# Attention with the output projection folded into the value weights on the chip

## The chip, the cores and the metric

The kernel runs on one core of one Trainium2 chip. The metric is the device time of one execution in microseconds; the median of three runs is given. Profiles come from one further execution, recorded by the hardware profiler. TensorE is written PE (its weight loads PEld), VectorE DVE, ScalarE ACT, GpSimd POOL and SyncE SP, as the profile has them. A matmul of 32-bit numbers leaves two records in the trace.

## The reference

The program is four layers on an image x of 48 channels and 128 x 128 points; each layer normalises x in groups of three channels, computes something and adds it to x. Only the first layer is touched:

```python
def _L0_conv_ref(x, qkv_w, dw_w, proj_w, temperature):
    qkv = jnp.einsum('bchw,oc->bohw', x, qkv_w)
    qkv = jax.lax.conv_general_dilated(qkv, dw_w, window_strides=(1, 1), padding='SAME', feature_group_count=3 * c, ...)
    q, k, v = jnp.split(qkv, 3, axis=1)
    q, k, v = (tok(q), tok(k), tok(v))          # 16384 tokens of 48 channels
    q = _l2norm(q)
    k = _l2norm(k)
    attn = jnp.einsum('bnc,bmc->bnm', q, k) * temperature
    attn = jax.nn.softmax(attn, axis=-1)
    out = jnp.einsum('bnm,bmc->bnc', attn, v)
    out = out.transpose(0, 2, 1).reshape(b, c, h, w)
    return jnp.einsum('bchw,oc->bohw', out, proj_w)
```

x becomes x plus this, of the normalised x. The other layers are recurrent sweeps over the image, a layer with Fourier transforms of 8 x 8 patches, and a state-space scan over tokens. The projection is linear in v, and v is linear in the value weights; the division by the softmax's sum is one number for each query.

## The kernel before

Everything is 32-bit. The layers run one after the other (`tile_kernel`). The image stays in SBUF in two large tiles, xa and xb; in attention xa holds the image and then the queries, and xb holds the keys k and the values v.

**Setup and convolution** (`attention`). The channels are laid out with a gap: 48 channels lie in rows 0 to 31 and 33 to 48 of 64 (GAP is 49), so that row or column 32 can hold ones. Line 129 builds proj, 128 x 112, from two DMAs (lines 131 to 133): in each half of 64 rows the projection stands in columns 0 to 47, and row 32, which carries the sum of the softmax, has ones in columns 64 to 111. `packed_weights` (line 106) multiplies 1x1 weights and 3x3 weights into one tile wt, 128 partitions, four groups, 192 columns: 64 each for q, k, v. Then VectorE takes the statistics of x (line 155). The convolution runs in eight bands of 16 rows, each in two steps of eight rows: `band` normalises on VectorE and places shifted copies by DMAs on SP, `conv` multiplies on TensorE, and `take` divides q and k by their norms and turns v by transposes through PSUM tile pt. Line 269 copies v out on VectorE; GpSimd writes ones into row 32 of k (line 272) and column 32 of v (line 273).

**Attention** (`attend`, chosen at run time for a small temperature; `attend_shifted` is the other branch and isn't run with these inputs). Queries go in 32 chunks of 512 (variable c), keys in 64 steps of two tiles of 128 (variable j). `scores` issues four matmuls, each in a quarter of the array, into one of three PSUM buffers s, and ScalarE takes the exponential into e. `sums` multiplies e with v, again four quarters of 64 columns, into acc, which has one buffer. Sums stand two steps behind their scores (BEHIND). The operations of TensorE and ScalarE are kept in the order of the program by the wrapper `InOrder`, which is why all of them carry line 48 in the profile; VectorE, GpSimd and SP are ordered by the scheduler of the kernel language.

**A chunk end** (class `Finish`) has two parts. When the last sums of a chunk are issued, `__init__` loads the residual xres by SP (line 357), copies acc to o on ScalarE, and adds the two halves of its free dimension on VectorE into osum (line 361). The two halves of partitions are still separate. In the next chunk, after the step j = 6, `result` multiplies proj with osum: that one product adds the halves of partitions, projects, and spreads the softmax's sum over 48 rows. Its output takes a turn of the buffers s. ScalarE copies it to y, and VectorE takes the reciprocal (line 369), multiplies (370), adds the residual (371) and takes the statistics for the next layer (372); SP stores x1 (373). After the last chunk `result` follows `__init__` at once, and the next layer, `sweeps`, begins with the statistics.

Of the kernel before, what the change touches and what calls it, by code (L numbers as in the profile page):

```python
# [19 lines left out]
F32 = mybir.dt.float32  # L20
# [6 lines left out]
C = 48  # L27
H = W = 128
N = H * W
CH = 512  # L30
GAP = 49
# [68 lines left out]
def packed_weights(nc, pool, name, w, dw, cols):  # L100

    w1 = pool.tile([128, 4, cols], F32, name="w1")
    nc.scalar.dma_start(w1.rearrange("c t o -> c (t o)"), w)
    wt = pool.tile([128, 4, cols], F32, name=name)
    nc.scalar.dma_start(wt.rearrange("c t o -> c (t o)"), dw)
    nc.vector.tensor_mul(wt, wt, w1)
    return wt
# [6 lines left out]
def attention(ctx, tc, xq, other, x1, const, ins):  # L114


    nc = tc.nc
    ident, blk, st = const["ident"], const["blk"], const["st"]
# [3 lines left out]
    kv = ctx.enter_context(tc.tile_pool(name="l0_kv", bufs=1))  # L122

    k = other[:, 0:HALF]

    v = other[:, HALF:N].rearrange("p (t c) -> p t c", c=64)


    proj = kv.tile([128, 64 + C], F32, name="proj")
    nc.vector.memset(proj, 0.0)  # L130
    for b in (0, 64):
        nc.sync.dma_start(proj[b : b + GAP, 0:C], ins["l0_proj"])
        nc.vector.memset(proj[b + 32 : b + 33, 64:], 1.0)
    temp = kv.tile([128, 1], F32, name="temp")
    nc.sync.dma_start(temp, ins["l0_temp"].to_broadcast([128, 1]))

# [3 lines left out]
    absT = kv.tile([128, 1], F32, name="absT")  # L140
    nc.vector.tensor_mul(absT, temp, sgn)

    with ExitStack() as a:
# [6 lines left out]


        wt = packed_weights(nc, wp, "wt", ins["l0_w"], ins["l0_dw"], 192)

        for i in range(NQ):
            nc.vector.bn_stats(st[:, i, :], xq[0:C, i * CH : (i + 1) * CH])
# [79 lines left out]
        def take(t0, p, pv):  # L235

            sqs, psss, nrms = [], [], []
            for n in range(2):
                sqs.append(sp.tile([128, CH], F32, name="sq"))
                act.activation(sqs[n], p[n], AF.Square)  # L240
            vt = sp.tile([128, CH], F32, name="vt")
            act.copy(vt, pv)

            for n in range(2):
                psss.append(ps2.tile([128, CH], F32, name="pss"))
                pe.matmul(psss[n], lhsT=blk, rhs=sqs[n], start=True, stop=True)
                nrms.append(sp.tile([128, CH], F32, name="nrm"))
                act.activation(nrms[n], psss[n], AF.Sqrt)
            pt = ps1.tile([128, 4, 2, 64], F32, name="pt")
            for i in range(4):  # L250
                pe.transpose(
                    pt[:, i].rearrange("t n c -> t (n c)"), vt[:, i * 128 : (i + 1) * 128], ident
                )
            kb = 64 * (t0 // HALF)
            tk = t0 % HALF
            left = []
            for n in range(2):
                nc.vector.tensor_scalar_max(nrms[n], nrms[n], 1e-12)
                rn = sp.tile([128, CH], F32, name="rn")
                nc.vector.reciprocal(rn, nrms[n])  # L260
                q = slice(t0 + n * CH, t0 + (n + 1) * CH)
                nc.vector.scalar_tensor_tensor(
                    xq[0:64, q], p[n][0:64], sgn[0:64], rn[0:64], ALU.mult, ALU.mult
                )
                left.append(q)
                nc.vector.tensor_mul(  # L266
                    k[kb : kb + 64, tk + n * CH : tk + (n + 1) * CH], p[n][64:128], rn[64:128]
                )
            nc.vector.tensor_copy(
                v[:, t0 // 128 : t0 // 128 + 8, :].rearrange("t (n i) c -> t i n c", n=2), pt  # L270
            )
            nc.gpsimd.memset(k[kb + 32 : kb + 33, tk : tk + 2 * CH], 1.0)
            nc.gpsimd.memset(v[:, t0 // 128 : t0 // 128 + 8, 32:33], 1.0)
            return left

        cur = band(0)
# [17 lines left out]
    small = nc.values_load(absT[0:1, 0:1].bitcast(mybir.dt.int32))  # L294
    bits = int(np.float32(32.0).view(np.int32))
    with tc.If(small <= bits) as near:
        attend(tc, xq, k, v, x1, proj, absT, st, ins)
    with near.Else():
        attend_shifted(tc, xq, k, v, x1, proj, absT, ident, st, ins)


@with_exitstack
def attend(ctx, tc, xq, k, v, x1, proj, absT, st, ins):

    nc = tc.nc
    act, pe = InOrder(tc, nc.scalar), InOrder(tc, nc.tensor)  # L310
    NQ = N // CH
    KT = N // 2 // 128
    BEHIND = 2

    ep = ctx.enter_context(tc.tile_pool(name="l0_e", bufs=BEHIND + 3))
    sp = ctx.enter_context(tc.tile_pool(name="l0_b", bufs=2))
    ps_s = ctx.enter_context(tc.tile_pool(name="l0_ps", bufs=3, space=PSUM))
    ps_a = ctx.enter_context(tc.tile_pool(name="l0_pa", bufs=1, space=PSUM))


    sides = [slice(0, 64), slice(64, 128)]
    quarters = [(part, half, to) for part in sides for half, to in enumerate(sides)]

    def scores(c, j):
        s = ps_s.tile([128, 2, CH], F32, name="s")
        for part, half, _ in quarters:
            b = 64 * half
            pe.matmul(
                s[part, half, :],
                lhsT=k[b : b + GAP, j * 128 + part.start : j * 128 + part.stop],  # L330
                rhs=xq[b : b + GAP, c * CH : (c + 1) * CH],
                start=True,
                stop=True,
            )
        e = ep.tile([128, 2, CH], F32, name="e")
        act.activation(e, s, AF.Exp, scale=absT)
        return e

    def sums(acc, j, e):

        for part, half, to in quarters:
            pe.matmul(
                acc[to, part.start // 64, :],
                lhsT=v[part, half * KT + j, :],
                rhs=e[part, half, :],
                start=(j == 0),
                stop=(j == KT - 1),
            )

    class Finish:  # L350


        def __init__(self, c, acc):
            self.c = c
            self.cols = slice(c * CH, (c + 1) * CH)
            self.xres = sp.tile([C, CH], F32, name="xres")
            nc.sync.dma_start(self.xres, ins["x"][:, self.cols])
            o = sp.tile([128, 2, CH], F32, name="o")
            act.copy(o, acc)
            self.o = sp.tile([128, CH], F32, name="osum")  # L360
            nc.vector.tensor_add(self.o, o[:, 0], o[:, 1])  # L361

        def result(self):
            p = ps_s.tile([128, 2, CH], F32, name="s")[0 : 64 + C, 0, :]
            pe.matmul(p, lhsT=proj, rhs=self.o, start=True, stop=True)
            y = sp.tile([64 + C, CH], F32, name="y")
            act.copy(y, p)
            rec = sp.tile([C, CH], F32, name="rec")
            nc.vector.reciprocal(rec, y[64 : 64 + C])  # L369
            nc.vector.tensor_mul(rec, y[0:C], rec)  # L370
            nc.vector.tensor_add(xq[0:C, self.cols], rec, self.xres)
            nc.vector.bn_stats(st[:, self.c, :], xq[0:C, self.cols])
            nc.sync.dma_start(x1[:, self.cols], xq[0:C, self.cols])

    waiting, finish, acc = [], None, None
    for c in range(NQ):
        for j in range(KT):
            waiting.append((c, j, scores(c, j)))

            if c and j == BEHIND:  # L380
                continue
            while len(waiting) > BEHIND:
                n, i, e = waiting.pop(0)
                if i == 0:
                    acc = ps_a.tile([128, 2, CH], F32, name="acc")
                sums(acc, i, e)
                if i == KT - 1:
                    finish = Finish(n, acc)
            if c and j == BEHIND + 4:
                finish.result()  # L390
    for n, i, e in waiting:
        sums(acc, i, e)
    Finish(NQ - 1, acc).result()


@with_exitstack
def attend_shifted(ctx, tc, xq, k, v, x1, proj, absT, ident, st, ins):

    nc = tc.nc
    NQ = N // CH  # L400
# [11 lines left out]
    k16 = k16p.tile([128, HALF], F16, name="k16")  # L412
    for i in range(0, HALF, 2048):
        nc.vector.tensor_copy(k16[:, i : i + 2048], k[:, i : i + 2048])

    class Shift:

# [45 lines left out]
    class Finish:  # L463
# [9 lines left out]

        def result(self):
            p = ps_1.tile([128, CH], F32, name="pmisc")
            nc.tensor.matmul(p[0 : 64 + C], lhsT=proj, rhs=self.o, start=True, stop=True)
            rec = sp.tile([C, CH], F32, name="rec")
            nc.vector.reciprocal(rec, p[64 : 64 + C])
            nc.vector.tensor_mul(rec, p[0:C], rec)
            nc.vector.tensor_add(xq[0:C, self.cols], rec, self.xres)  # L480
            nc.vector.bn_stats(st[:, self.c, :], xq[0:C, self.cols])
            nc.sync.dma_start(x1[:, self.cols], xq[0:C, self.cols])
# [1216 lines left out]
```

## Time and profile before

| | us |
|---|---|
| median of three runs | 7702.65 (7696.43 to 7703.76) |
| the profiled execution's own time | 7707.8 |
| its span in the trace | 7706.0 |
| setup and convolution | 0 to 257 |
| attention | 257 to 3821 |
| chunk ends in it | 32 |
| product with proj, start to start of the next | 1.04 |
| copy of acc (128 x 1024) on ScalarE | 1.00 |
| addition osum (128 x 512) on VectorE | 0.69 |
| reciprocal (48 x 512) on VectorE | 3.35 |
| exponential (128 x 1024) on ScalarE | 1.11 |

Over the whole span PE is busy for 6227.8 us (81%), DVE for 3377.0 (44%), ACT for 4455.4 (58%) and POOL for 2793.0 (36%). A line of the timeline has the start in us from the span's start, the length, the engine, the line of the code, the operation, the tiles that are written and read with the shapes, the number of instructions merged, and in brackets how long the engine was idle before and what ended that. Neighbouring instructions of a kind are merged into one line, and since matmuls overlap in the array, lines of PE overlap too; the distance of two starts is then the measure, not the length. Tile p of `result` is allocated under the name s, so that the product with proj reads `s<-osum,proj`.

### The profile page before, as it was taken

What the parts mean: (1) busy time and instruction counts of PE and PEld (TensorE: products, weight loads), DVE (VectorE), ACT (ScalarE), POOL (GpSimd) and SP (SyncE); (2) the same over time, 40 slices, a digit from 0 to 9 for tenths busy, and PEclk for the clock granted to TensorE, in tenths of its full rate; (3) what the DMA queues carried; (4) which work ended last, traced back from release to release, by engine and by line L of the source; (5) the groups of instructions that cost most, each with busy time, mean ns of one, the idle gap of its engine ahead of it and who ended that gap; (6) DMA issues with size and microseconds to landing.
All of it is one profiled execution on the core that took longest, in us unless ns stands there. A gap on an engine that the chain in (4) does not pass through costs nothing. (4 is left out here: it accounts for less than half of the span.)

```text
span 7706.0 us, 203399 instructions
## 1 busy us (share of the span) xinstructions
PE 6227.8 (81%) x93872; PEld 3159.4 (41%) x93872; DVE 3377.0 (44%) x2467; ACT 4455.4 (58%) x4928; POOL 2793.0 (36%) x573
## 2 busy tenths in 40 slices
PE   7999999999999999999888889745545554554555
PEld 2333333333333333333377755334434343434444
DVE  8300000000000000000022234489999999999998
ACT  2566666666666666666624014366666666666665
POOL 1000000000000000000000122289999999999998
PEclk9999999999999999999999999867767767676676
DMA  5000000000000000000000011166556656666775
GB/s 76 10 3 3 3 2 3 3 3 2 3 3 3 2 3 3 2 3 3 6 1 17 1 31 48 23 166 166 158 160 161 157 161 154 163 157 161 180 180 148
DMA packets 167597, 488.84 MB, mean 63 GB/s; under 512 B 33440, under 2 KB 51968, under 8 KB 163984
## 3 DMA queue, kind: packets, MB, share of 16 engines
q1 hardware_dynamic: 160704, 470.30, 24.3%
q8 instruction: 737, 12.08, 0.7%
q10 hardware_dynamic: 6032, 5.44, 0.3%
q14 instruction: 124, 1.02, 0.0%
HBM read 428.86 MB, written 22.02 MB: 59 GB/s over the span
## 5 line engine op out<-in xcount | busy, mean ns | idle before, releaser
L48 ACT ACTIVATE e<-s,absT 128x1024 f32<-128x1024 f32 x2048 | 2277.3, 1114 | 1217.9 <-PE s L48 1217.9
L1459 POOL TENSOR_TENSOR h<-du,bt 128x3072 f32<-128x3072 f32 (+1 forms) x386 | 2559.5, 6666 | 102.7 <-DMA du<-rep 70.2
L48 PE MATMUL s<-xa,xb 49*64 49x512 f32 x16384 | 2128.4, 589 | 10.6 <-DVE xb L266 10.6
L48 PE MATMUL acc<-e,xb 64*64 64x512 f32 x16384 | 2125.0, 588 | 0.0
L1466 DVE TENSOR_TENSOR_SCAN h<-dA,carry,h 128x1024 f32<-128x1024 f32 x864 | 1940.7, 2329 | 48.9 <-ACT dA L48 32.9
L48 ACT ACTIVATE dA<-dt,a 128x1024 f32<-128x1024 f32 x1152 | 1287.2, 1118 | 864.0 <-DVE h L1466 854.5
L48 PE MATMUL y<-h,cw 128*32 128x48 f32 x49152 | 899.2, 246 | 949.0 <-issue 511.9
L361 DVE TENSOR_TENSOR osum<-o 128x512 f32<-128x512 f32 x32 | 22.2, 692 | 3114.8 <-ACT o L48 3114.8
L593 POOL MEMSET xa<- 48x128 f32 x1 | 0.3, 326 | 3561.0 <-PE acc L48 3561.0
L48 PEld LDWEIGHTS y<-h,cw 128*32 128x32 f32 x49152 | 809.9, 140 | 1072.3 <-issue 661.8
L48 PEld LDWEIGHTS s<-xa,xb 49*64 49x64 f32 x16384 | 626.3, 132 | 1151.2 <-issue 615.6
L48 PEld LDWEIGHTS acc<-e,xb 64*64 64x64 f32 x16384 | 628.6, 132 | 1133.7 <-issue 1111.2
L1466 DVE TENSOR_TENSOR_SCAN h<-dA,h 128x1024 f32<-128x1024 f32 x288 | 636.1, 2272 | 44.1 <-ACT dA L48 33.6
L48 PE MATMUL yz<-ev,sel 128*8 128x48 f32 x4096 | 192.9, 260 | 277.2 <-ACT ev L48 273.3
L48 PEld LDWEIGHTS yz<-ev,sel 128*8 128x8 f32 x4096 | 162.5, 106 | 334.9 <-ACT ev L48 308.7
L657 PE MATMUL p<-xb,w 112*112 112x129 f32 x1524 | 235.7, 291 | 42.2 <-DVE xb L48 42.1
L657 PE MATMUL p<-xa,w 112*112 112x129 f32 x1524 | 233.5, 289 | 41.8 <-DVE xa L48 41.8
L678 POOL TENSOR_TENSOR xb<-xb,xa 48x2048 f32<-48x2048 f32 (+2 forms) x10 | 44.6, 4464 | 563.0 <-DVE xa L48 563.0
L657 PEld LDWEIGHTS p<-xb,w 112*112 112x112 f32 x1524 | 183.7, 178 | 93.9 <-DVE xb L48 93.9
L640 ACT COPY xa<-xb 48x128 f32<-48x128 f32 x256 | 107.4, 419 | 196.6 <-issue 138.1
L657 PEld LDWEIGHTS p<-xa,w 112*112 112x112 f32 x1524 | 181.8, 177 | 93.3 <-DVE xa L48 93.3
L369 DVE RECIPROCAL rec<-y 48x512 f32<-48x512 f32 x32 | 107.1, 3348 | 257.5 <-ACT y L48 257.5
(187 smaller groups left out, 3602.4 us busy)
## 6 DMA issues: line engine op xcount, KB each, us to landing
du<-rep SPq DMA_DIRECT2D x768, 256.0 KB
dt<-rep SPq DMA_DIRECT2D x768, 256.0 KB
rest<-xa SPq DMA_DIRECT2D x96, 77.0 KB
rest<-band SPq DMA_DIRECT2D x48, 129.9 KB
rep<-dd SPq DMA_DIRECT2D x24, 192.0 KB
yd<-ys ACTq DMA_DIRECT2D x256, 12.0 KB
band<-band SPq DMA_DIRECT2D x8, 414.4 KB
xa<-xa SPq DMA_DIRECT2D x16, 199.1 KB
```

The lines of the kernel that those rows point to most:

```text
L48: ins = method(*args, **kwargs).ins
L361: nc.vector.tensor_add(self.o, o[:, 0], o[:, 1])
L369: nc.vector.reciprocal(rec, y[64 : 64 + C])
L593: nc.gpsimd.memset(b[64:K, lines, E + W - 1 : E + W], 0.0)
L640: nc.scalar.copy(u[at : at + C, :, y], t[0:C, E + h, E : E + W])
L657: nc.tensor.matmul(p, lhsT=w[0:K, which, i, :], rhs=state[0:K, 2 * i : 2 * i + L], start=False, stop=(i == 2),)
L678: nc.gpsimd.tensor_add(xr, xr, u[0:C, x : x + xr.shape[2], E : E + H].rearrange("c w h -> c h w"),)
L1459: nc.gpsimd.tensor_mul(h[:, p, ks], du.unsqueeze(1).to_broadcast([128, ks.stop - ks.start, LC]), r["bt"][:, ks],)
L1466: nc.vector.tensor_tensor_scan(h[:, p, k, :], dA, h[:, p, k, :], carry[:, i, k : k + 1] if ci else 0.0, ALU.mult, ALU.add,)
```

## The change

The value weights are multiplied by the projection once, at the start: four transposes, a copy, four matmuls and a copy back into columns 128 to 191 of wt. Values then come out of the convolution already projected, in columns 0 to 47 without a gap, and GpSimd writes ones into columns 48 to 63. Rows 0 to 47 of acc are then the projected output and rows 48 to 63 sixteen copies of the softmax's sum, in both halves of partitions. In a chunk end VectorE adds the halves of the free dimension, copies the upper 64 partitions down, and adds them; it takes the reciprocal of partitions 32 to 63, and three DMAs on SP copy its rows 48 to 63 to rows 0 to 47 of another tile. All of that is in `__init__`. `result` multiplies, adds the residual, takes statistics and stores, with no product and no work of ScalarE. proj is 64 x 64 and comes by one DMA. The branch that isn't run gets a small matrix add in place of proj.

```diff
-    proj = kv.tile([128, 64 + C], F32, name="proj")
+    proj = kv.tile([64, 64], F32, name="proj")
     nc.vector.memset(proj, 0.0)
-    for b in (0, 64):
-        nc.sync.dma_start(proj[b : b + GAP, 0:C], ins["l0_proj"])
-        nc.vector.memset(proj[b + 32 : b + 33, 64:], 1.0)
+    nc.sync.dma_start(proj[0:GAP, 0:C], ins["l0_proj"])
...
         wt = packed_weights(nc, wp, "wt", ins["l0_w"], ins["l0_dw"], 192)
+
+        values = wt[:, :, 128:192]
+        turned = wp.tile([64, 4, 128], F32, name="turned")
+        pt = ps1.tile([128, 4, 2, 64], F32, name="pt").rearrange("c t n o -> c t (n o)")
+        for t in range(4):
+            pe.transpose(pt[0:64, t, :], values[:, t, :], ident)
+        act.copy(turned, pt[0:64])
+        pt = ps1.tile([128, 4, 2, 64], F32, name="pt")
+        for t in range(4):
+            pe.matmul(pt[:, t, 0, :], lhsT=turned[:, t, :], rhs=proj, start=True, stop=True)
+        act.copy(values, pt[:, :, 0, :])
...
-            nc.gpsimd.memset(v[:, t0 // 128 : t0 // 128 + 8, 32:33], 1.0)
+            nc.gpsimd.memset(v[:, t0 // 128 : t0 // 128 + 8, C:64], 1.0)
...
             act.copy(o, acc)
-            self.o = sp.tile([128, CH], F32, name="osum")
-            nc.vector.tensor_add(self.o, o[:, 0], o[:, 1])
+            both = sp.tile([128, CH], F32, name="both")
+            nc.vector.tensor_add(both, o[:, 0], o[:, 1])
+            second = sp.tile([64, CH], F32, name="second")
+            nc.vector.tensor_copy(second, both[64:128])
+            self.y = sp.tile([64, CH], F32, name="y")
+            nc.vector.tensor_add(self.y, both[0:64], second)
+
+            rec = sp.tile([64, CH], F32, name="rec")
+            nc.vector.reciprocal(rec[32:64], self.y[32:64])
+            self.rec = sp.tile([C, CH], F32, name="recs")
+            for i in range(0, C, 64 - C):
+                nc.sync.dma_start(self.rec[i : i + 64 - C], rec[C:64])
 
         def result(self):
-            p = ps_s.tile([128, 2, CH], F32, name="s")[0 : 64 + C, 0, :]
-            pe.matmul(p, lhsT=proj, rhs=self.o, start=True, stop=True)
-            y = sp.tile([64 + C, CH], F32, name="y")
-            act.copy(y, p)
-            rec = sp.tile([C, CH], F32, name="rec")
-            nc.vector.reciprocal(rec, y[64 : 64 + C])
-            nc.vector.tensor_mul(rec, y[0:C], rec)
-            nc.vector.tensor_add(xq[0:C, self.cols], rec, self.xres)
+            y = self.y[0:C]
+            nc.vector.tensor_mul(y, y, self.rec)
+            nc.vector.tensor_add(xq[0:C, self.cols], y, self.xres)
             nc.vector.bn_stats(st[:, self.c, :], xq[0:C, self.cols])
             nc.sync.dma_start(x1[:, self.cols], xq[0:C, self.cols])
```

More of the change, by code (lines that the diff above doesn't have):

```diff
@@ L296, in attention, with attend @@
     with tc.If(small <= bits) as near:
-        attend(tc, xq, k, v, x1, proj, absT, st, ins)
+        attend(tc, xq, k, v, x1, absT, st, ins)
     with near.Else():
-        attend_shifted(tc, xq, k, v, x1, proj, absT, ident, st, ins)
+        attend_shifted(tc, xq, k, v, x1, absT, ident, st, ins)
 @with_exitstack
-def attend(ctx, tc, xq, k, v, x1, proj, absT, st, ins):
+def attend(ctx, tc, xq, k, v, x1, absT, st, ins):
     nc = tc.nc
@@ L396, in attend_shifted @@
 @with_exitstack
-def attend_shifted(ctx, tc, xq, k, v, x1, proj, absT, ident, st, ins):
+def attend_shifted(ctx, tc, xq, k, v, x1, absT, ident, st, ins):
     nc = tc.nc
@@ L414, in attend_shifted @@
         nc.vector.tensor_copy(k16[:, i : i + 2048], k[:, i : i + 2048])
+    add = sp.tile([128, 64 + C], F32, name="add")
+    nc.vector.memset(add, 0.0)
+    for b in (0, 64):
+        nc.vector.tensor_copy(add[b : b + C, 0:C], ident[b : b + C, b : b + C])
+        nc.vector.tensor_copy(
+            add[b + 32 : b + 64, 64:], ident[b + 32 : b + 64, b + C : b + C + 1].to_broadcast([32, C])
+        )
     class Shift:
@@ L475, in result @@
             p = ps_1.tile([128, CH], F32, name="pmisc")
-            nc.tensor.matmul(p[0 : 64 + C], lhsT=proj, rhs=self.o, start=True, stop=True)
+            nc.tensor.matmul(p[0 : 64 + C], lhsT=add, rhs=self.o, start=True, stop=True)
             rec = sp.tile([C, CH], F32, name="rec")
```

## The prediction

> **What bounds the kernel now.** I read the busy table of the whole page first, then a table of busy times by stretch, the stretches cut where the timeline shows a stage to end: setup and convolution, first attention chunk, attention, its last chunk, its tail, and the later layers.
>
> ```profile
> core 0: us, PE busy (x) PEld busy (x) DVE busy (x) ACT busy (x) POOL busy (x), PEclk, DMA share, GB/s
> 0.00:257.00 257.00, 203.34 (x644) 75.51 (x644) 214.77 (x197) 65.68 (x114) 26.52 (x40) 0.97 0.45 63
> 257.00:374.00 117.00, 116.74 (x1056) 46.12 (x1060) 0.11 (x1) 75.64 (x70) 0.95 (x1) 0.97 0.01 3
> 374.00:3712.00 3338.00, 3338.00 (x30780) 1179.17 (x30780) 182.80 (x150) 2175.80 (x1980) 0.00 (x0) 1.00 0.01 3
> ...
> 3821.00:3845.00 24.00, 2.37 (x9) 1.45 (x10) 8.07 (x12) 10.57 (x11) 15.27 (x8) 0.56 0.13 36
> ...
> 4900.00:7706.00 2806.00, 1512.59 (x54516) 1142.42 (x54514) 2629.36 (x1241) 1773.82 (x2122) 2593.50 (x408) 0.69 0.61 157
> ```
>
> The columns are named in the first line. In the 3338 us of attention (257 to 3821 with both ends) TensorE is never idle and runs at the full granted clock, 1.00. ScalarE is busy 65% of it, VectorE 5%, GpSimd not at all, the DMA engines 1%. So a product saved there is time saved, and work put on VectorE or on the queues is beside it. Next the timeline of TensorE through one chunk end:
>
> ```profile
> 2493.70 1.04 PE L48 MATMUL s<-xa,xb 49*64 49x512 f32 x8
> 2494.56 1.04 PE L48 MATMUL acc<-e,xb 64*64 64x512 f32 x8
> 2495.53 1.11 PE L48 MATMUL s<-osum,proj 128*112 128x512 f32 x2
> 2496.57 1.09 PE L48 MATMUL s<-xa,xb 49*64 49x512 f32 x8
> 2497.48 1.04 PE L48 MATMUL acc<-e,xb 64*64 64x512 f32 x8
> 2498.34 1.04 PE L48 MATMUL s<-xa,xb 49*64 49x512 f32 x8
> ```
>
> A group of eight records starts 0.86 us after the one before it (2493.70, 2494.56), so one pass over a key tile (scores and sums) is 1.72 us. The product with proj breaks that: without it the next scores would start at 2494.56 + 0.86 = 2495.42; they start at 2496.57, 1.15 later, and the sums after them come 0.91 and not 0.86 behind. The product costs TensorE 1.15 + 0.05 = 1.20 us. Its own waits on VectorE are not in this: it is placed when osum is long there. Check by the whole: osum starts at 485.43 (second chunk) and at 3712.42 (thirty-first), 3226.99 us for 29 chunks, 111.28 each; 64 passes of 1.72 make 110.08; the difference is again 1.20. Nothing else at a chunk end costs TensorE time: two score groups, then two sum groups, keep it fed while ScalarE copies acc.
>
> The last view is the end of attention, where no product hides anything:
>
> ```profile
> 3820.70 1.01 ACT L48 COPY o<-acc 128x1024 f32<-128x1024 f32 x1 [1.38 <-PE acc L48]
> ...
> 3821.75 0.69 DVE L361 TENSOR_TENSOR osum<-o 128x512 f32<-128x512 f32 x1 [94.81 <-ACT o L48]
> 3822.59 1.08 PE L48 MATMUL s<-osum,proj 128*112 128x512 f32 x2 [1.95 <-DVE osum L361]
> 3823.70 0.58 ACT L48 COPY y<-s 112x512 f32<-112x512 f32 x1 [1.99 <-PE s L48]
> 3824.32 3.35 DVE L369 RECIPROCAL rec<-y 48x512 f32<-48x512 f32 x1 [1.88 <-ACT y L48]
> 3827.70 0.68 DVE L370 TENSOR_TENSOR rec<-y,rec 48x512 f32<-48x512 f32 x1
> 3828.48 0.68 DVE L371 TENSOR_TENSOR xa<-rec,xres 48x512 f32<-48x512 f32 x1
> 3829.19 0.31 SPq L373 DMA_DIRECT2D x<-xa  x1
> 3829.20 0.69 DVE L372 BATCH_NORM_STATS2 st<-xa 48x6 f32<-48x512 f32 x1
> ```
>
> From the copy of acc to the end of the statistics is 3829.89 - 3820.70 = 9.19 us, and the next layer's normalisation needs those statistics: this chain is on the path once.
>
> [...]the products of 64 columns run four at a time, the one with proj fills the array, and there are 0.11 us ahead of it (2495.42 to 2495.53) and, with two records of 0.43 each (a score group's 0.86 over its two rounds of four), 0.18 behind it. [...]two residual loads issued from 257.25 on are waited for until 259.49, 2.2 us. [...]the trace shows copies between exponentials without a reload.[...]
>
> **The change part by part.**
> *Steady chunk ends.* result() runs 31 times inside the stream of passes. Removed from TensorE: 31 x 1.20 = 37.2 us, all on the path. At the least it is the bare start-to-start 1.04 (2495.53 to 2496.57), 32.2[...]; no more than 37.2, since the passes themselves don't change: v still has 64 columns. Also removed: the copy of the product on ScalarE, 0.58 us of 111, worth nothing, as ScalarE already waits 0.6 us for every score tile; and a turn of the three score buffers, for which no wait ends late in TensorE's stream.
> *Added to VectorE* at each chunk end: a 64x512 copy in SBUF (not in the trace in this shape; the 128x512 tensor_scalar of line 258 takes 0.36, a copy out of PSUM 0.69, I take 0.36) and an add, 0.69. The reciprocal of 32 partitions stays at 3.35, as 48 and 128 partitions both take it. That is 1 us more in a VectorE that is idle 95% of the time. *Added to SP*: three DMAs of 32 KB between reciprocal and multiply. Queued behind them on SP are the store of x1 and the next residual load, which has a chunk, 111 us, to arrive; queued behind the multiply on VectorE is only this chunk's add and statistics. The chain, 10 to 12 us, is hidden by 110 us of passes. TensorE and ScalarE wait for none of it. If that cover went (a chunk shorter than the chain) each end would cost the chain.
> *The tail*, once. Copy of acc: sums start 1.05 later as now. First add 0.69, copy 0.36, add 0.69, with some 0.04 between: the reciprocal starts 2.9 after the copy of acc instead of 3.62 and ends at 6.3. Then the three DMAs: an issue each 0.35 (the store and the residual load at 388 stand 0.36 apart), the last issued 0.7 after the first, and about 2.1 to land: 9.1. Multiply, add, statistics take 2.2 as now (3827.70 to 3829.89): 11.3. Against 9.19 that is +2.1. The bounds: landing 1.45 after the last issue, as the earlier of readings at 257.25 allows, gives about +1.4; 3.05, the largest wait from an issue's end (39.48 to 42.53, the shifted copies of the convolution), and longer issues of 0.6, give +4. No gain, for the DMA alone outlasts the 1.1 of product and 0.6 of copy.
> *Setup.* Four transposes, four products, two ScalarE copies and one load of proj instead of two. The weights are ready at 12.5 (line 106 starts at 11.55 and takes 0.96); the transposes at 0.27 and products at 0.6 take 3.5, the copies 0.6 each, waits between engines under 1: done near 18, or 20 if proj, issued at 10.87, lands late. ScalarE is next needed at 32.48 for the square root, TensorE at 30.95, the weights at 42.5; VectorE's statistics until 29.85 cover it. If that cover were gone it would cost 6 to 8 us. Cost 0; if a table load fell between the copies and the square root, 1.28 us (line 85). Setting the ones in v is wider: 16 columns instead of one on GpSimd (line 273), 0.12 becoming some 0.2 to 0.3 once in 12.3 us. Behind it on that queue is the setting of k's ones (line 272), which waits 1.26 us for VectorE anyway; 0. The other branch (large temperature) isn't run.
> *Sum*: -37.2 + 2.1 + 0 = -35.1 us. Against the profiled execution, 7707.8 around a span of 7706.0, that is 7672.7. The median of the runs is 7702.65, 0.07% under it; the same subtraction gives **7667.6**.
>
> **The rivals.**
> (a) *Saved time comes back as a wait for exponentials.* For it: right at the chunk end ScalarE does the copy of acc and two exponentials in a row, and the product gave it 1.2 us of grace. Against: those are over 7 us before the product stands in the stream, and sums run two passes behind their scores. It would leave only the tail: 7702.65 + 2.1 = 7705.
> (b) *Slower: the granted clock.* 15 columns of v that held zeros hold ones, and every sum product of the whole stage toggles them[...]. It would show from the first chunk on. At 0.97, what the first chunk's stretch was granted, 3564 us of stage would grow by 3564 x (1/0.97 - 1) = 110: 7778. It decides from a clock of 0.986 down: the 50 us to 7718 (0.2% over) are then used up. Against: 1.00 through the whole stage with TensorE always busy; lower clocks stand in the trace only where TensorE idles (0.56 in the tail, 0.69 in the last layer, busy half the time).
> (c) *Half the gain.* The later layers are ordered engine by engine and wait on each other within microseconds; a shift of stores and waits, a late first pass[...] could take 15 to 20 us: 7685. The last 2806 us contain such loose ends (short issue gaps on the chain that ended last), but nothing in them reads anything that the change moves.
> That the change doesn't do what it says can't be: the diff leaves no product in the chunk end.
>
> **How the numbers follow.** Forecast 0.84 (7668), (c) 0.04, (a) 0.05, (b) 0.04, something slower that I do not see 0.03. A measurement of this kernel can tell about 0.2%, 15 us, from no change. Faster: the forecast and half of (c), 0.86; same: the rest of (c), (a) and a part of the unseen, 0.08; slower: (b) and the rest, 0.06. Range: downward 7702.65 - 37.2 + 1.4 = 7667 less the 6 us that the lowest run lies under the median, and 3 because the median of the new runs scatters too, 7658; upward 7702.65 - 32.2 + 4 + 1.3 = 7676, a microsecond for run scatter, and on to (c), 7687. (a) and (b) stay out.
>
> **What would show it.** Right: osum's successor starts every 110.1 us; the stretch 374 to 3712 holds no other product than s and acc and stays at clock 1.00; all records of the new DMAs lie between reciprocal and multiply; the tail from the copy of acc to the statistics takes 10.5 to 13 us; the first convolution product still starts near 42.5. Wrong: a chunk period over 110.5, a wait of TensorE for ScalarE or VectorE at chunk ends, a clock under 0.99 in attention, or later layers (3845 to the end, 3861 us) that take another time than before.

## The result, and the profile after

The changed kernel takes 7669.62 us (median of six, 7663.18 to 7674.91) against 7701.84 for the kernel before, beside it: a ratio of 0.9959, 95% interval 0.9946 to 0.9972. Forecast were 7667.6 and a range of 7658 to 7687. The number is right. The sum behind it is right in its main term only: two terms were missed, one of +12.9 us at the end of attention and one of about -7 to -11 us in the last layer, and they nearly cancel.

This is the table of busy times by stretch of the changed kernel, whose attention ends earlier (the columns are named in its first line):

```profile
core 0: us, PE busy (x) PEld busy (x) DVE busy (x) ACT busy (x) POOL busy (x), PEclk, DMA share, GB/s
...
374.00:3680.00 3306.00, 3306.00 (x30760) 1219.34 (x30755) 217.85 (x211) 2160.90 (x1953) 0.00 (x0) 1.00 0.02 4
...
4864.00:7668.00 2804.00, 1526.90 (x54569) 1147.38 (x54567) 2631.66 (x1246) 1779.66 (x2132) 2596.52 (x411) 0.69 0.61 157
```

TensorE is still never idle in attention and its clock is still 1.00, with ones in 15 columns that held zeros. VectorE has risen from 183 us in 3338 to 218 in 3306, and nothing waits for it. Here is TensorE around the place where the product stood, at the second chunk end:

```profile
488.66 1.05 PE L48 MATMUL acc<-e,xb 64*64 64x512 f32 x8
489.52 1.05 PE L48 MATMUL s<-xa,xb 49*64 49x512 f32 x8
490.38 1.05 PE L48 MATMUL acc<-e,xb 64*64 64x512 f32 x8
```

The starts are 0.86 apart, with no break. The chain of a chunk end on VectorE runs meanwhile; the last line is the start of the next chunk's:

```profile
480.70 0.69 DVE L368 TENSOR_TENSOR both<-o 128x512 f32<-128x512 f32 x1 [99.19 <-ACT o L48]
481.43 0.42 DVE L370 COPY second<-both 64x512 f32<-64x512 f32 x1
...
489.35 0.68 DVE L382 TENSOR_TENSOR y<-y,recs 48x512 f32<-48x512 f32 x1 [3.40 <-DMA recs<-rec]
...
590.78 0.69 DVE L368 TENSOR_TENSOR both<-o 128x512 f32<-128x512 f32 x1 [99.24 <-ACT o L48]
```

From 480.70 to 590.78 is 110.08 us, 64 passes of 1.72 and nothing more. The move of the upper 64 partitions (`second<-both`) takes 0.42 here. In the tail, the end of the last chunk, it does not:

```profile
3780.05 1.01 ACT L48 COPY o<-acc 128x1024 f32<-128x1024 f32 x1 [1.41 <-PE acc L48]
...
3780.49 13.91 POOL L610 MEMSET xb<- 32x16512 f32 x1
3781.10 0.69 DVE L368 TENSOR_TENSOR both<-o 128x512 f32<-128x512 f32 x1 [97.40 <-ACT o L48]
3781.82 12.85 DVE L370 COPY second<-both 64x512 f32<-64x512 f32 x1
...
3798.80 1.79 SPq L378 DMA_DIRECT2D recs<-rec  x3
3802.11 0.68 DVE L382 TENSOR_TENSOR y<-y,recs 48x512 f32<-48x512 f32 x1 [3.34 <-DMA recs<-rec]
...
3803.60 0.69 DVE L384 BATCH_NORM_STATS2 st<-xa 48x6 f32<-48x512 f32 x1
```

The tail, from the copy of acc to the end of the statistics, is 3804.29 - 3780.05 = 24.24 us, where it was 9.19. The same copy that takes 0.42 in every other chunk is 12.85 long, with no wait in front of it: its time is counted as busy. It ends (3794.67) 0.27 after GpSimd's fill ends (3794.40), the MEMSET that prepares xb for the next layer. In the kernel before, the same fill ran beside the tail and delayed nothing there, since VectorE had no copy in it:

```profile
3820.73 13.91 POOL L589 MEMSET xb<- 32x16512 f32 x1 [1.21 <-PE acc L48]
```

The spans of the two profiled executions, 7706.0 and 7668.4, differ by 37.6. By place: attention begins at 254.70 and not 257.26 (-2.6); from there to the copy of the last acc -38.1; the tail +15.05; from the last product of the third layer's output (4958.9, now 4932.3) to the last store of the image (7703.1, now 7665.5), that is in the last layer, 2744.2 became 2733.2 (-11.0); all else -1.0.

### The profile page after: what moved, and what is told of

Read it like the earlier page. It is cut to its first block, busy times and chain, and to the rows that moved or that the text cites. A ratio compares the mean times of both kernels' runs of the same rounds, so it can differ in the third digit from the quotient of the medians.

```text
span 7668.4 us, 203495 instructions
## 1 busy us (share of the span) xinstructions
PE 6195.4 (81%) x93820; PEld 3198.7 (42%) x93820; DVE 3423.7 (45%) x2529; ACT 4439.4 (58%) x4899; POOL 2794.9 (36%) x573
## 4 chain that ended last, share of the span: by engine, by line
PE 61%; DVE 23%; issue 6%; POOL 3%; DMA 2%; ACT 2%; SPq 0%; DVEq 0%; ACTq 0%; POOLq 0%
PE s L48 23%; PE acc L48 23%; DVE h L1487 20%; PE p L678 6%; PE y L48 3%; POOL h L1480 3%; PE pc L816 2%; DMA du<-rep 1%; DVE xa L48 1%; DVE xb L48 1%; PE pp L48 1%; PE po L873 1%; PE f L842 1%; ACT dA L48 1%; PE pc L825 1%
## 5 line engine op out<-in xcount | busy, mean ns | idle before, releaser
L1487 DVE TENSOR_TENSOR_SCAN h<-dA,carry,h 128x1024 f32<-128x1024 f32 x864 | 1940.3, 2327 | 38.9 <-ACT dA L48 24.2
L368 DVE TENSOR_TENSOR both<-o 128x512 f32<-128x512 f32 x32 | 22.2, 692 | 3192.1 <-ACT o L48 3192.1
L48 PEld LDWEIGHTS s<-xa,xb 49*64 49x64 f32 x16384 | 650.6, 132 | 1122.7 <-issue 583.5
L48 PEld LDWEIGHTS acc<-e,xb 64*64 64x64 f32 x16384 | 649.8, 132 | 1112.2 <-issue 1089.3
L816 PE MATMUL pc<-wt,xa 128*128 128x288 f32 x768 | 210.9, 426 | 6.1 <-DVE xa L93 6.1
## 6 DMA issues: line engine op xcount, KB each, us to landing
du<-rep SPq DMA_DIRECT2D x768, 256.0 KB
dt<-rep SPq DMA_DIRECT2D x768, 256.0 KB
```

Of the source, the lines that this page charges most:

```text
L48: ins = method(*args, **kwargs).ins
L368: nc.vector.tensor_add(both, o[:, 0], o[:, 1])
L816: nc.tensor.matmul(pc[i], lhsT=xp[:, r0 + i, dx : dx + W], rhs=wt[:, dx, :], start=(dx == 0), stop=(dx == 2 and i == 1 and last),)
L1487: nc.vector.tensor_tensor_scan(h[:, p, k, :], dA, h[:, p, k, :], carry[:, i, k : k + 1] if ci else 0.0, ALU.mult, ALU.add,)
```

## The experiments

**The form of the move.** In the changed kernel, the copy becomes a maximum of the tile with itself, an operation of two inputs:

```diff
-            nc.vector.tensor_copy(second, both[64:128])
+            nc.vector.tensor_tensor(second, both[64:128], both[64:128], ALU.max)
```

> The changed kernel with one instruction of its chunk end in another form: the 64x512 move of the upper partitions is a maximum of the tile with itself (a two-input operation) in place of a copy. Theory: in the tail the copy took 12.85 us because it wanted something that GpSimd held during its 13.91 us fill of xb, and the two-input form doesn't want it. Then the move takes 0.69, the tail from the copy of acc to the statistics falls from 24.2 to 11.9 us, and the time is 12.3 under the changed kernel's 7669.6: 7657. The steady chunk period stays 110.08. Rival: the delay belongs to the place or the data (a dependence on GpSimd's fill, both ends of it waiting), not to the form; then the move still ends with the fill, the tail stays near 24, 7670.

Measured: 7658.52 (7648.49 to 7660.36), ratio to the kernel before 0.9936, interval 0.9923 to 0.9950. Its tail:

```profile
3780.24 13.91 POOL L610 MEMSET xb<- 32x16512 f32 x1
...
3781.58 0.69 DVE L370 TENSOR_TENSOR second<-both 64x512 f32<-64x512 f32 x1
```

The move takes 0.69 in the middle of the fill, and the tail is 3791.89 - 3779.81 = 12.08. The copy's form is what waits, not the place.

**The same copy in the kernel before.** The kernel before with a copy that nobody reads:

```diff
             nc.vector.tensor_add(self.o, o[:, 0], o[:, 1])
+            second = sp.tile([64, CH], F32, name="second")
+            nc.vector.tensor_copy(second, self.o[64:128])
```

> The kernel before with one instruction added to each chunk end: a 64x512 copy on VectorE of the upper partitions of osum, not used. Theory: 31 of them take 0.42 beside the stream and cost nothing; the last one starts after GpSimd's fill of xb has begun and waits for its end, near 3834.7, so that the reciprocal behind it starts some 10.5 us later. Time 7701.8 + 10.5 = 7712. Rival: the 12.85 us of the changed kernel came from something else in its tail; then the copy takes 0.42 there too, the reciprocal isn't late, and the time stays 7702.

Measured: 7713.46 against 7703.46, ratio 1.0014 (1.0007 to 1.0020). In its tail:

```profile
3816.66 13.91 POOL L591 MEMSET xb<- 32x16512 f32 x1 [1.21 <-PE acc L48]
...
3818.40 12.45 DVE L363 COPY second<-osum 64x512 f32<-64x512 f32 x1
...
3819.95 0.59 ACT L48 COPY y<-s 112x512 f32<-112x512 f32 x1 [2.30 <-PE s L48]
...
3830.78 3.33 DVE L371 RECIPROCAL rec<-y 48x512 f32<-48x512 f32 x1
```

The reciprocal begins at 3830.78, 10.2 us after the product's result was out of ScalarE (3820.54). One instruction whose output nobody uses, held by the fill, costs 10 us in a kernel that otherwise is as before. With the run above that shows the cause from both sides: a copy on VectorE beside a fill on GpSimd. The three runs agree: the copy lasts to the end of the fill (12.85 and 12.45 us), while the maximum and the addition beside the fill, at 3781.10 in the changed kernel, take 0.69. What it is in GpSimd's fill that holds the copy, no trace shows.

The trace of the kernel before has the same wait, small, in the very row that the prediction took its price from. Line 258 ran 32 times in the convolution, from 0.36 to 1.27 us, and line 272 is a MEMSET of GpSimd:

```profile
85.90 0.94 POOL L272 MEMSET xb<- 1x1024 f32 x1 [1.26 <-DVE xb L266]
86.21 0.92 DVE L258 TENSOR_SCALAR nrm<-nrm 128x512 f32<-128x512 f32 x1 [0.43 <-ACT nrm L48]
...
111.02 0.43 DVE L258 TENSOR_SCALAR nrm<-nrm 128x512 f32<-128x512 f32 x1
111.11 1.22 POOL L272 MEMSET xb<- 1x1024 f32 x1 [1.26 <-DVE xb L266]
```

At 86.21 VectorE came second and ended 0.29 after the MEMSET; at 111.11 GpSimd came second, and its MEMSET took 1.22 and not 0.94. (At 135.39 the two begin within 0.04 us of each other, and VectorE takes 1.27.) The usual 0.36 to 0.43 hides this; the row's longest time shows it.

**The product back.** In the changed kernel, a product with the identity's first 112 columns, in chunks 0 to 30, whose output nobody uses (`attend` is handed the identity):

```diff
-            both = sp.tile([128, CH], F32, name="both")
+            both = self.both = sp.tile([128, CH], F32, name="both")
...
         def result(self):
+            if self.c < NQ - 1:
+                p = ps_s.tile([128, 2, CH], F32, name="s")[0 : 64 + C, 0, :]
+                pe.matmul(p, lhsT=ident[:, 0 : 64 + C], rhs=self.both, start=True, stop=True)
             y = self.y[0:C]
```

> The changed kernel with a product of 128x112 by 128x512 put back after step j = 6 of 31 chunks; its output is not used. All else, the chain on VectorE and the DMAs too, stays. Theory: the gain is the product's 1.20 us on TensorE, so the chunk period goes from 110.08 back to 111.28, and the time rises by 31 x 1.20 = 37.2 to 7707, over the kernel before. Rival: the gain came from the shorter chain of ScalarE, the score buffers or from later layers; then the period rises by clearly less than 1.2 (none if the product fits into gaps), 7670 to 7690.

Measured: 7718.59 (7710.87 to 7727.82), ratio 1.0019 (1.0012 to 1.0027). The period:

```profile
481.41 0.69 DVE L368 TENSOR_TENSOR both<-o 128x512 f32<-128x512 f32 x1 [100.40 <-ACT o L48]
...
592.69 0.69 DVE L368 TENSOR_TENSOR both<-o 128x512 f32<-128x512 f32 x1 [100.44 <-ACT o L48]
```

It is 111.28 again, as expected, and attention from its first scores to its last is 37.3 us longer than in the changed kernel (3559.4 against 3522.1). But the median rose by 49 and not by 37, against the 7707 expected. The profile has the rest in the last layer: 2750.8 us by the same two marks as above, against 2733.2, though the order of instructions there is the same on every engine. That is 17.6 and not 12, but the profiled execution was one of the slower, 6.3 over the median.

**Folding alone.** Setup and values as in the changed kernel, chunk ends as before, with a fixed matrix of zeros and ones in place of proj (the one that the diff builds for the other branch):

```diff
...
+            p = ps_s.tile([128, 2, CH], F32, name="s")[0 : 64 + C, 0, :]
+            pe.matmul(p, lhsT=add, rhs=self.o, start=True, stop=True)
...
```

> Folded value weights as in the changed kernel, but chunk ends as before: a product with a fixed 0/1 matrix adds the halves and spreads the sum, ScalarE copies it out, reciprocal of 48 partitions. Theory: the setup lies under the statistics of x and the ones in v cost nothing, so the time is that of the kernel before, 7702 within 4, chunk period 111.28, tail 9.2. Rival: folding itself moves the time (the changed kernel's attention began 2.6 us earlier, and its later layers took 11 us less in the profile); then 7688 to 7699.

Measured: 7699.66, ratio 0.9995 (0.9986 to 1.0003). No difference that can be told: the gain is not in the folding itself but in what it lets the chunk ends leave out. The earlier begin of attention isn't the change's either: in the kernel before with the copy it is 254.0, in this one 256.0.

**A longer chain.** In the changed kernel:

```diff
-            nc.vector.reciprocal(rec[32:64], self.y[32:64])
+            for _ in range(4):
+                nc.vector.reciprocal(rec[32:64], self.y[32:64])
```

> The changed kernel with the reciprocal of each chunk end done four times instead of once, which puts 3 x 3.35 = 10 us more on VectorE ahead of the DMAs, 32 times. Theory: the chain of a chunk end lies under 110 us of products, so 31 of these cost nothing, the chunk period stays 110.08, and only the tail grows by 10: 7669.6 + 10 = 7680. Rival: something in the stream of products waits for the chain (the queries' tile that the result is written to, the residual's buffers, SP's queue); then a part of 320 us shows, and the period grows.

Measured: 7679.03 (7675.67 to 7687.90), ratio 0.9974 (0.9964 to 0.9984). The period is 110.08 (482.58 to 592.66); the tail is 3816.30 - 3781.94 = 34.4, 10.1 more. In the 31 chunk ends under the stream 310 us of work on VectorE cost nothing; in the last one 10 us cost 10.

**Small products in the setup.** These ask whether the last layer's time depends on how many instructions TensorE has had before it. Three are the changed kernel with 16, 31 or 64 products of 64x64 by 64, where TensorE waits for proj; one is the kernel before with 40. Their output isn't used. The edit with 31:

```diff
+        pad = ps1.tile([128, CH], F32, name="pv")
+        for t in range(31):
+            pe.matmul(pad[0:64, 0:64], lhsT=ident[:, 0:64], rhs=ident[:, 0:64], start=True, stop=True)
```

> The changed kernel with 31 small products (64x64 by 64) on TensorE in the setup, where it waits for proj for 13.45 us; their output isn't used. The kernel with the product put back took 12 us more than the 37.2 of its 31 products, and its trace has them in the last layer, whose instructions are the same. Theory: the last layer's time depends on where TensorE's instructions lie, which 31 more of them shift as in that kernel; then this one takes some 12 us more than the changed kernel's 7669.6, 7681, all in the last layer. Rival: the 12 us have nothing to do with the number of instructions ahead of them; then 7670 within 4.

> The changed kernel with 16 small products in the setup, a quarter of the distance of the gaps; output unused. Theory of the borders: somewhere between the two times known, 7670 and 7681, in the last layer alone. Rival (more instructions ahead cost more): half of 11, 7675. It tells little between the two; it is made for the curve.

> The changed kernel with 64 small products in the setup in place of the 31 of the earlier run; output unused. TensorE's trace in the last layer has an idle gap of 2 to 4 us after every 128 records at which it waits for nothing that the profile shows, and instructions come in blocks of 16 KB by the page (12.08 MB in 737 packets). Theory: what matters is where the blocks' borders fall among the products; 64 products are 128 records, one whole distance of the gaps, so the borders fall as without them, and the time is the changed kernel's, 7670. Rival: more instructions ahead cost more, or any filler in the setup does; then 7681 or above.

> The kernel before with 40 small products in the setup, where TensorE waits 31 us for the statistics; output unused. The changed kernel has 24 products fewer ahead of the later layers than the kernel before (32 gone, 8 new), which is 40 more but for a whole distance of 64. Theory of the borders: the last layer then runs as in the changed kernel, some 8 to 10 us faster than in the kernel before, and the time is 7692 to 7694, though nothing was taken out. Rival (more instructions cost more, or the last layer's difference has another source in the change): 7702 or above.

| kernel | us | ratio to before (interval) | last layer in the profile | instructions ahead |
|---|---|---|---|---|
| changed | 7669.62 | 0.9959 (0.9946 to 0.9972) | 2733.2 | 0 |
| changed + 16 | 7675.75 | 0.9963 (0.9949 to 0.9977) | 2739.5 | 64 |
| changed + 31 | 7680.93 | 0.9973 (0.9962 to 0.9984) | 2743.1 | 124 |
| changed + 64 | 7672.82 | 0.9959 (0.9946 to 0.9973) | 2734.4 | 256 |
| before | 7701.77 | 1 | 2744.2 | 132 |
| before + 40 | 7694.41 | 0.9990 (0.9983 to 0.9997) | 2731.2 | 292 |

Each ratio is to runs of the kernel before that were taken beside it. The last column counts TensorE's instructions in the trace ahead of the layer (products, weight loads and waits), as the number by which they exceed the changed kernel's.

The products themselves are hidden: with 31 of them attention begins at 253.9. TensorE in the last layer of the changed kernel:

```profile
5573.74 1.56 PE L48 MATMUL y<-h,cw 128*32 128x48 f32 x128 [1.42 <-issue]
5578.31 0.69 PE L48 MATMUL y<-h,cw 128*32 128x48 f32 x19 [3.00 <-issue]
```

There is an idle gap after 128 records in which nothing is waited for that the profile shows (it writes `issue`), and this recurs through the layer: 188 such gaps are over 0.8 us, 0.86 to 4.89 long, and from one to the next it is 128 records (62 times) or, but for one or two records, a multiple of 128. 128 matmul records and their 128 weight loads are 256 instructions, called a block here, and its end a border. The profile's page of the kernel before counts 737 packets and 12.08 MB in one instruction queue, 16.4 KB each, and 93872 matmul records and as many weight loads on TensorE, which in blocks of 256 would be 733. That a block is such a packet is an estimate from these two counts; no trace shows a packet beside a gap.

The traces also show where the gaps stand. Number TensorE's records within the last layer: with 64 more products, one block, 169 of the changed kernel's 188 gaps over 0.8 us are at the same records. With 16 most of them stand 32 records earlier, with 31 they stand 62 earlier and in the kernel before 66, always half the number in the last column. So the gaps belong to the stream of instructions and not to the layer's work.

The times go the same way. With 64 products no difference can be told. With 31 the median is 11 us higher, though the two intervals overlap. In the kernel before, 40 products gain 7.4 us with nothing removed. They were meant to bring the borders to where the change brings them (32 products gone, 8 new: 24 fewer) and bring them within 18 records: a transpose leaves one record and not two (the four in the setup are x4 in the trace, the four products x8), and the removed products took 28 waits with them. The rivals (more instructions cost more, or a cause inside the change) expected neither of these two results. Over all twelve kernels' profiles the layer takes 2729 to 2738 us where the last column, less whole blocks, is 0 to 36, and 2736 to 2751 where it is 64 to 159. The two groups touch, and at 155 (the product back) and 159 (folding alone) it took 2750.8 and 2736.2, so single executions scatter by as much as the effect. That the borders move is shown; that they make the difference in time is likely. The run with 16 tells nothing by itself, as was expected.

**A product in the last chunk alone**, with the maximum in the others; VectorE takes the reciprocal from PSUM (the building of `add` is left out here):

```diff
+            if c == NQ - 1:
+                p = ps_s.tile([128, 2, CH], F32, name="s")[0 : 64 + C, 0, :]
+                pe.matmul(p, lhsT=add, rhs=both, start=True, stop=True)
+                self.y = sp.tile([64, CH], F32, name="y")
+                act.copy(self.y[0:C], p[0:C])
+                self.rec = sp.tile([C, CH], F32, name="recs")
+                nc.vector.reciprocal(self.rec, p[64 : 64 + C])
+                return
...
```

> The changed kernel with the move as a two-input maximum, and with the last chunk alone ended by a product with a 0/1 matrix, whose sums VectorE takes from PSUM for its reciprocal while ScalarE copies the rest: no move, no DMA and no copy in the tail. Theory: the tail falls from the 12.1 us of the kernel with the maximum to 8.6, all else stays, and the time is 7655, under both kernels. Rival: the two DMA-free steps wait for the same fill or for ScalarE, and the tail stays at 12 or more, 7658 or above.

Measured: 7652.18 (7652.08 to 7660.76), ratio 0.9942 (0.9928 to 0.9955). The tail is 3788.77 - 3778.97 = 9.8, not 8.6:

```profile
3782.64 0.58 ACT L48 COPY y<-s 48x512 f32<-48x512 f32 x1 [2.65 <-PE s L48]
3783.25 3.36 DVE L384 RECIPROCAL recs<-s 48x512 f32<-48x512 f32 x1 [2.54 <-ACT y L48]
```

The product took 1.75, after 1.95 of idle time, and the reciprocal came behind ScalarE's copy of the same tile rather than beside it. That part of the rival was right. This kernel and the one with the maximum have the lowest medians, and none of their runs reaches the changed kernel's lowest, 7663.18, though the intervals of their ratios still overlap with its own. Between the two no difference can be told.

## Why the prediction was right, point by point

*Steady chunk ends*, -37.2: right, and shown by putting the product back (+37.3 in attention, period 111.28) and by the period without it (110.08). The 0.11 us ahead of the product and the 0.18 behind it went with it.

*VectorE and SP beside the stream*, 0: right. Four reciprocals in place of one left the period at 110.08. The copy takes 0.42 where 0.36 was assumed. The issues stand 0.6 apart and not 0.35 (three in 1.79), hidden as well.

*The tail*, +2.1: wrong in two parts. The term "copy 0.36" was priced from the short instances of line 258, with GpSimd at rest, though the same row has longer ones beside a MEMSET and the fill stood in the tail of the trace of before: 12.85 where 0.36 was put. And the DMAs took 3.31 from first issue to use instead of 2.8, because of the slower issues. Without the collision, in the kernel with the maximum, the tail is +2.9 on 9.19, inside the range given for it (+1.4 to +4); with it +15.05, far outside.

*Setup*, 0: right in its outcome, by less than was said. The products waited for proj, issued on SP after the loads of x, until 27.34, when all was to be done by 18 or 20. And a table was loaded between the copies and the square root; the prediction had named this and priced it at 1.28:

```profile
27.34 1.93 PE L48 MATMUL pt<-proj,turned 64*128 64x64 f32 x8 [13.45 <-DMA proj<-in_l_proj_dram]
...
29.70 1.28 ACT L85 ACT_TABLE_LOAD   x1
```

The load ended at 30.98 and the square root began at 32.99: 2 us of cover were left.

*Later layers*, 0: wrong. Nothing in them reads what moves, as was argued, but TensorE has 132 instructions fewer ahead of them, and so the borders of its blocks fall elsewhere, by 66 records; that this is the cause is likely and not proven. The two executions shown differ by 11.0 there; the medians with and without 40 products in the kernel before differ by 7.4.

So the sum should have been -37.2 + 15.05 and some -7 to -11: -29 to -33, and -32.2 was measured. Forecast were -35.1. That they are close is partly luck. One of the prediction's signs of being right failed, a tail of 10.5 to 13 us, and one of being wrong came true, later layers that take another time than before.

Of the rivals, (a), a wait for exponentials, and (b), a lower clock, are refuted by the gapless stream and the clock of 1.00. (The prediction's remark that lower clocks stand only where TensorE idles doesn't fit its own table: the first chunk has 0.97, with TensorE busy for 116.74 of 117 us.) (c), half the gain, named the later layers, and a shift of this size is real; its sign was on our side this time. What stays open is how a block's border would cost the last layer its time. The scan on VectorE in that layer waits less for its decay factors, tile dA (the 864 scans that carry a state on: idle 24.2 us for it in the changed kernel, 32.9 before, and 41.9 in 846 of them with the product back), but no run follows single borders to these waits.

## What to carry to other kernels

In a stage where one engine is never idle, its start-to-start times can give the gain of a removed instruction closely (1.20 us forecast and measured here), and other engines' work can be free there (310 us on VectorE were); the price is paid at the ends of the stage, so read there what every other engine is doing at that moment. Price a copy on VectorE beside a long fill on GpSimd at what is left of the fill (12.85 and 12.45 us here, where 0.42 is usual); another form of the same move may avoid it (the maximum took 0.69). In a row of the profile, read the longest time too and not the mean alone. Differences of 0.1% in a part of the kernel whose instructions didn't change may come from where the instruction blocks end (40 products in the setup gained 7.4 us of 7702 here): add a block's worth of fillers (64 products here), and half of one, before explaining them.

## What was not expected of the hardware

A 64x512 copy took 0.42 us alone and 12.85 beside a GpSimd fill, and the profile shows that as a busy VectorE, not as a wait. With 31 small products hidden in the setup the median rose by 11 us, and the profile has 10 of them in a layer that begins 4900 us later; with 64 it rose by 3, which is no more than these runs scatter.
